# Four PSUM banks for the products of a four-layer graph network, attention weights written over the softmax tile, and three smaller edits

## The chip, the core and the metric

The kernel runs on one core of a Trainium2 chip. Five engines with queues of their own work side by side: TensorE (PE) multiplies into PSUM, VectorE (DVE) and ScalarE (ACT) read PSUM and work on SBUF, GpSimd (POOL) works on SBUF alone, and SyncE (SP) issues the DMA transfers. [...] Each queue is worked off in order, so an instruction that waits holds up all that stand behind it on its engine.

The metric is the device time of one execution in microseconds (us). One execution was also recorded by the hardware profiler.

## The reference

The input `x` is 128 graphs of 64 nodes with 512 features, with one 64x64 adjacency `adj` for all. Four layers follow each other; each is `x = x + f(relu(layernorm(x)))`:

```
L0: softmax(q kT / 8 + mask) v                       8 heads of 64
L1: (softmax(q kT / 8 + mask) v) Wo + bo             8 heads of 64
L2: rel = adj.T * (q kT); rel / ||rel|| over j; rel v    one head of 512
L3: o = (softmax(masked q kT / 8) v) Wp + bp;  o + layernorm(o)
```

All arithmetic is float32. Nearly all of it is in the projections of 512x512 weights.

## The kernel before

**Tiles.** The 8192 rows are worked in 16 tiles of 512 rows per layer, 64 tiles in all; `n` counts them through the four layers. Between layers the rows go through DRAM.

**Projections (`projection`, lines 526 to 565).** A 512x512x512 projection is seven products of half size (a Strassen scheme) where the plain way has eight. The sums of weight blocks are made once per weight (`load_w`, `sums_w`, lines 343 to 363), those of the activation, `S` and `SO`, once per tile (`sums_x`, line 497, mostly on POOL). One product is four matmuls, 128x128 by 128x256. A float32 matmul is two passes and so two rows in the trace: a product is eight rows. The seven products stand in the order 1, 6, 5, 2, 7, 3, 4 and use four PSUM tiles ("homes"): products 1 and 2 the first, 6 and 7 the second, 5 and 3 the third, 4 the fourth. Products 2, 7 and 3 add onto what is in their home, after the first of the pair has been read once. The readers are ACT copies (`s1`, `z5`, `Y11`) and DVE additions (`u2`, `u3`, `Y12`, `Y21`); POOL makes `Y22` from SBUF.

**PSUM (lines 287 to 289).** [...] The homes turn through a ring of three tiles of a bank, `ps_mm` (names `mm` in the profile). Scores and attention products have two tiles of two banks (`so`). One bank, `ps_t` (`t`), is for the warm-up, the matrix folding and layer 2's `relate`. A ring (`Ring`, line 196) hands out its tiles in turn, and a user waits until the readers of the former user of that tile are done.

**Attention (`attend`, `finish0`, `finish13`).** Two score tiles `s` per `n` go through mask and maximum (DVE), subtraction (POOL), exponential (ACT), sum (DVE) and scaling (POOL). They are then transposed by `turn` (line 447): DVE splits the float32 values into two 16-bit planes, `zp`; a transposing DMA writes `hp`; ACT puts the planes together, here into `aT`. The normalised input takes the same way into `hT`. `zp` is a ring of four tiles, `hp` of three, `s` and `aT` of two each, and `z` (used in `fold` and in `tail3`, the layer norm of layer 3's output) of two.

**Start.** 22 transposes of the identity (`WARM`, line 302) run on PE while the first rows load. The first tile (`n == 0`, lines 478 to 487) is transposed on PE, in four groups of four, one for each 128 rows.

**Folding (`fold`, lines 404 to 426).** From n = 3 on the matrices of layer 2 are folded (`Wq.T Wk` and the transposed `Wv`) in pieces between the other work; the raw weights come in three loads of 1 MB.

**End.** The last tile's output projection is done as plain matmuls, four tiles of 128 rows (lines 1060 to 1080), each followed by its layer norm and store.

**What sets the order.** The code doesn't issue instructions. `Plan` (line 56) records steps with their reads, writes and an estimated duration (line 225); generators such as `attend` are advanced one step per product by a clock of ticks (`spawn`, `tick`, `run`, lines 936 to 953). `Plan.order` (line 131) then plays the steps through: when an engine is free it takes, of the steps that are ready, the one recorded first, with those that read an `mm` tile counted as 60 steps earlier (`RUSH`). The result is the fixed order of each engine's queue. All instructions are issued in line 193, so the profile names that line for all of them, and groups are told apart by their tiles.

Of the kernel before, what the change touches and what calls it, by code (L numbers as in the profile page):

```python
# [18 lines left out]
P = 128  # L19
# [240 lines left out]
def gnn_stack_kernel(  # L260
# [17 lines left out]
    def pool(name, bufs, **kw):  # L278
        return Ring(ctx.enter_context(tc.tile_pool(name=name, bufs=1, **kw)), bufs)
# [4 lines left out]
    rows = pool("rows", 3)  # L284
    sm = pool("sm", 4)
    dram = ctx.enter_context(tc.tile_pool(name="dram", bufs=1, space=bass.MemoryType.DRAM))
    ps_mm = pool("ps_mm", 3, space=bass.MemoryType.PSUM)
    ps_so = pool("ps_so", 2, space=bass.MemoryType.PSUM)
    ps_t = pool("ps_t", 1, space=bass.MemoryType.PSUM)


    ident = const.tile([P, P], F32, tag="ident", name="ident")
# [4 lines left out]
    gps.memset(mhalf, -0.5)  # L297


    pw = ps_t.tile([P, KC, P], F32, tag="t", name="pw")  # L300
    for i in range(WARM):
        pe.transpose(pw[:, i % KC, :], ident, ident)

# [39 lines left out]
    def load_w(name, src):  # L343

        w = wp.tile([P, 7, 2, H2], F32, tag="w", name=name)
        b12 = p2.tile([P, 2, H2], F32, tag="b12", name=f"b12_{name}")

        def part(i, j):
            return src[i * H2 : (i + 1) * H2, j * H2 : (j + 1) * H2].rearrange("(c p) f -> p c f", p=P)

        dma(w[:, W11], part(0, 0))
        dma(w[:, W21], part(1, 0))
        dma(b12, part(0, 1))
        dma(w[:, W22], part(1, 1))
        return w, b12

    def sums_w(w, b12, eng):
        tt = eng.tensor_tensor
        tt(w[:, WT1], b12, w[:, W11], ALU.subtract)
        tt(w[:, WT2], w[:, W22], w[:, WT1], ALU.subtract)  # L360
        yield 1
        tt(w[:, WT4], w[:, W21], w[:, WT2], ALU.subtract)
        tt(w[:, WT3], w[:, W22], b12, ALU.subtract)

    W = {}

    def weight(name, src, eng=gps):
        got = load_w(name, src)
        W[name] = got[0]
        yield 4  # L370
        yield from sums_w(*got, eng)

    def now(gen):
        for _ in gen:
# [23 lines left out]

    def raw(tag, src, nm):
        t = p1.tile([P, KC, D], F32, tag=tag, name=nm)  # L400
        dma(t, src.rearrange("(c p) f -> p c f", p=P))
        return t

    def fold():

        rq, rk = raw("oT", wq2, "rq"), raw("SO", wk2, "rk")
        yield 8
        for dc in range(KC):
            pa = ps_t.tile([P, D], F32, tag="t", name=f"pfa_{dc}")
            plan.begin()  # L410
            for ec in range(KC):
                pe.matmul(pa, rq[:, ec, ts(dc, P)], rk[:, ec, :], start=(ec == 0), stop=(ec == KC - 1))
            plan.end()
            f = p2.tile([P, D], F32, tag="z", name=f"fa_{dc}")
            act.copy(f, pa)
            yield 1
            dma(a2d[dc * P : (dc + 1) * P, :], f)
            yield 1
        rv = raw("oT", wv2, "rv")
        yield 8  # L420
        for ec in range(KC):
            f = p2.tile([P, KC, P], F32, tag="z", name=f"ft_{ec}")
# [24 lines left out]
    def turn(dst, src, nm):  # L447


        zp = p4.tile([P, 2, D], U16, tag="zp", name=f"zp_{nm}")  # L450
        dve.tensor_copy(zp, src.bitcast(U16).rearrange("p (f w) -> p w f", w=2))
        hp = p3.tile([P, 2, KC, P], U16, tag="hp", name=f"hp_{nm}")
        plan.sync.dma_start(
            hp.rearrange("p w c t -> p (w c) t"), zp.rearrange("p w f -> p (w f)"), transpose=True
        )
        act.copy(dst.bitcast(U16).rearrange("p c (t w) -> p w c t", w=2), hp)

    def layer_norm(n):
        mv = sm.tile([P, NT, 2], F32, tag="mv", name=f"mv_{n}")
        rs = sm.tile([P, NT], F32, tag="rs", name=f"rs_{n}")  # L460
        nb = sm.tile([P, NT], F32, tag="nb", name=f"nb_{n}")

        def scales(at):
            pow_mhalf(rs[:, at], mv[:, at, 1], LN_EPS, f"{n}")
            dve.scalar_tensor_tensor(nb[:, at], mv[:, at, 0], -1.0, rs[:, at], ALU.mult, ALU.mult)

        for t in range(NT):
            stats(mv, t, xins[n][t], f"{n}")
            if n == 0:
                scales(slice(t, t + 1))  # L470
            if t % 2:
                yield 1
        if n:
            scales(slice(0, NT))
        yield 2
        hT = p2.tile([P, KC, T], F32, tag="hT", name=f"hT_{n}")
        hTs[n] = hT
        if n == 0:
            for t in range(NT):
                z = xins[n][t]  # L480
                act.activation(z, z, AF.Relu, bias=nb[:, t : t + 1], scale=rs[:, t : t + 1])
                pt = ps_mm.tile([P, KC, P], F32, tag="mm", name=f"pz_{n}_{t}")
                plan.begin()
                for c in range(KC):
                    pe.transpose(pt[:, c, :], z[:, ts(c, P)], ident)
                plan.end()
                (dve.tensor_copy if t else act.copy)(hT[:, :, ts(t, P)], pt)
        for t in range(NT) if n else ():
            z = xins[n][t]
            act.activation(z, z, AF.Relu, bias=nb[:, t : t + 1], scale=rs[:, t : t + 1])  # L490
            turn(hT[:, :, ts(t, P)], z, f"{n}_{t}")
            yield 1
        del xins[n]
        ready.add(("h", n))
        sums_of(n)
# [146 lines left out]
    def attend(n, qT, kT, v, done):  # L642
# [2 lines left out]
        plan.begin()  # L645
        psss = [scores(qT, kT, g, f"{n}_{g}") for g in range(2)]
        plan.end(300)
        ss = [p2.tile([P, 2 * KC, 2, G], F32, tag="s", name=f"s_{n}_{g}") for g in range(2)]
        yield 1
        for s, pss in zip(ss, psss):  # L650
            for b in range(2):
# [195 lines left out]
    def tail3(n, o):  # L847
# [111 lines left out]
    N = 4 * NB  # L959
    now(layer_norm(0))  # L960
    for name, got in zip(("q0", "k0"), first):
        W[name] = got[0]
        now(sums_w(*got, gps if name == "q0" else dve))
    now(weight("v0", wv0))
    make_masks()
    NAMES = {0: "qkv", 1: "qkv", 2: "av", 3: "qkv"}
# [6 lines left out]

    def want(name):
        spawn(weight(name, SRC[name]))

    pending = []

    def project(n):
# [5 lines left out]
        if m // NB == 1:  # L985
            run(projection(prod_N, W["o1"], sop, f"o_{m}", emit_out1(m)))
            spawn(tail1(m))
            if m == 2 * NB - 1:
                want("k3")
        else:  # L990
            ring, tag = (p1, "kT") if m < N - 2 else (wp, "w")
            o = ring.tile([P, NT, D], F32, tag=tag, name=f"o_{m}")
            run(projection(prod_N, W["o3"], sop, f"o_{m}", emit_out3(m, o)))
            spawn(tail3(m, o))

    for n in range(N):
# [50 lines left out]
        if l in (1, 3):  # L1047
            pending.append(n)
            spawn(load_xo(n), 4)
        if n == N - 4:  # L1050
            w12 = p2.tile([P, 2, H2], F32, tag="b12", name="w12")
            dma(w12, wp3[0:H2, H2:].rearrange("(c p) f -> p c f", p=P))

    while queue:
        tick()
    m = N - 1
    o3 = wp.tile([P, NT, D], F32, tag="w", name="o_last")
    mv = sm.tile([P, NT, 2], F32, tag="mv", name="mv_last")
    rs = sm.tile([P, NT], F32, tag="rs", name="rs_last")
    for t in range(NT):  # L1060
# [16 lines left out]
        a = p2.tile([P, D], F32, tag="z", name=f"a_last_{t}")  # L1077
# [38 lines left out]
```

## Time and profile before

| | |
|---|---|
| time, median of 3 runs | 2850.17 us (2849.34 to 2850.48) |
| the profiled execution's own time | 2849.34 us |
| its span, first to last instruction | 2847.6 us |
| busy: PE, DVE, POOL, ACT | 2829.3, 2039.3, 1847.4, 1246.9 us |
| one 128x256 pass on PE (group mean, with its pipeline) | 380 ns |
| DVE `zp<-s` / `zp<-xin` copy | 1488 / 979 ns, 188 and 252 of them |
| DVE `u<-mm,s` addition out of PSUM | 689 ns, 414 of them |
| transposing DMA `hp<-zp` | 444 issues, 3.1 us from issue to landing |

Passes on PE overlap, so the mean duration of one is longer than the time from one to the next. 168 passes that follow each other without a break take 36.53 us in the chain of waits: 0.217 us each. A product, eight passes, is thus 1.73 us. A wait is read as "who <- whom: total, times, longest". Windows of the span are given in us from its start.

### The profile page before, as it was taken

The page shows a single profiled execution, that of the slowest core. Times are in us where ns is not written, and L with a number is a line of the kernel's source. Part 1 is how long each engine was busy: PE and PEld are TensorE (multiplying, and loading weights), DVE is VectorE, ACT ScalarE, POOL GpSimd, SP SyncE. Part 2 cuts the span into 40 slices and gives each one's busy share as a digit, 9 for nine tenths or more (in the row PEclk, how much of TensorE's full clock was granted, in tenths as well). Part 3 has the DMA queues.
Part 4 walks back from the last instruction along what each step waited for, and adds up shares of the span by engine and source line. Part 5 has one row for each costly group of instructions (what it writes and reads, how often), then busy time and mean ns, then how long its engine had stood idle before and what let it go on. Part 6 is the DMA issues. An engine that isn't in the chain of part 4 may idle for free.

```text
span 2847.6 us, 61907 instructions
## 1 busy us (share of the span) xinstructions
PE 2829.3 (99%) x25822; PEld 2469.7 (87%) x25822; DVE 2039.3 (72%) x3104; ACT 1246.9 (44%) x1589; POOL 1847.4 (65%) x1349
## 2 busy tenths in 40 slices
PE   9999999999999999999999999999999999999998
PEld 8888888888888888888888888888888888888887
DVE  7677778877767667667666555555688788788787
ACT  4545555554443533534534443343444444444342
POOL 6456666656766667667677434344678688687786
PEclk9999999999999999999999999999999999999999
DMA  6666656556443433533546565656433433533531
GB/s 150 162 156 147 140 143 136 123 136 159 108 116 79 122 98 82 130 86 86 139 114 152 138 160 145 163 131 153 118 87 96 115 83 90 127 86 87 115 86 64
DMA packets 634746, 342.28 MB, mean 120 GB/s; under 512 B 485089, under 2 KB 566241, under 8 KB 634465
## 3 DMA queue, kind: packets, MB, share of 16 engines
q1 hardware_dynamic: 634464, 338.32, 49.1%
q8 instruction: 202, 3.31, 0.5%
q14 instruction: 80, 0.65, 0.1%
HBM read 152.61 MB, written 69.21 MB: 78 GB/s over the span
## 4 chain that ended last, share of the span: by engine, by line
PE 96%; DVE 2%; POOL 1%; issue 1%; DMA 0%; ACT 0%; POOLq 0%; DVEq 0%
PE mm L193 86%; PE so L193 8%; PE t L193 2%; DVE z L193 1%; DVE zp L193 0%; DVE st L193 0%; DVE xo L193 0%; POOL s L193 0%; DVE kT L193 0%; DMA hp<-zp 0%; DVE u L193 0%; POOL S L193 0%; DVE sr L193 0%; DMA xin<-in_x_dram 0%; DVE w L193 0%
## 5 line engine op out<-in xcount | busy, mean ns | idle before, releaser
L193 PE MATMUL mm<-S,w 128*128 128x256 f32 x3584 | 817.3, 380 | 3.7 <-DVE kT L193 1.3
L193 PEld LDWEIGHTS mm<-S,w 128*128 128x128 f32 x3584 | 678.2, 190 | 98.7 <-issue 2.6
L193 PE MATMUL mm<-hT,w 128*128 128x256 f32 x2688 | 631.8, 380 | 1.2 <-ACT xin L193 0.8
L193 DVE TENSOR_TENSOR u<-mm,s 128x512 f32<-128x512 f32 x414 | 285.2, 689 | 459.3 <-PE mm L193 303.8
L193 PEld LDWEIGHTS mm<-hT,w 128*128 128x128 f32 x2688 | 510.3, 190 | 72.1 <-ACT xin L193 1.0
L193 PE MATMUL mm<-w,S 128*128 128x256 f32 x2048 | 472.8, 381 | 1.9 <-DVE kT L193 1.4
L193 PEld LDWEIGHTS mm<-w,S 128*128 128x128 f32 x2048 | 385.2, 190 | 56.5 <-DVE kT L193 2.2
L193 ACT COPY hT<-hp 128x1024 uint16<-128x1024 uint16 x252 | 333.6, 1348 | 77.7 <-DMA hp<-zp 77.5
L193 PE MATMUL mm<-w,hT 128*128 128x256 f32 x1536 | 366.0, 381 | 0.0
L193 ACT COPY s<-mm 128x512 f32<-128x512 f32 x207 | 120.6, 583 | 523.8 <-PE mm L193 444.4
L193 POOL TENSOR_TENSOR s<-s,mx 128x1024 f32<-128x1024 f32 x96 | 184.4, 1922 | 239.6 <-DVE mx L193 239.5
L193 PEld LDWEIGHTS mm<-w,hT 128*128 128x128 f32 x1536 | 289.3, 190 | 41.2 <-ACT v L193 0.8
L193 ACT COPY aT<-hp 128x1024 uint16<-128x1024 uint16 x188 | 253.1, 1352 | 158.9 <-DMA hp<-zp 158.6
L193 POOL TENSOR_TENSOR xo<-xo,row 128x512 f32<-128x512 f32 x192 | 286.8, 1512 | 4.3 <-DMA xo<-x 4.3
L193 DVE COPY zp<-s 128x1024 uint16<-128x1024 uint16 x188 | 275.5, 1488 | 4.0 <-POOL s L193 3.8
L193 DVE COPY zp<-xin 128x1024 uint16<-128x1024 uint16 x252 | 242.7, 979 | 40.0 <-ACT xin L193 34.5
L193 ACT ACTIVATE xin<-xin,nb,rs 128x512 f32<-128x512 f32 x256 | 196.0, 808 | 97.5 <-DVE nb L193 93.6
L193 PE MATMUL mm<-w,SO 128*128 128x256 f32 x992 | 224.5, 379 | 0.0
L193 POOL TENSOR_TENSOR qT<-u,z 128x512 f32<-128x512 f32 x64 | 89.7, 1402 | 190.4 <-DVE u L193 172.7
L193 PEld LDWEIGHTS mm<-w,SO 128*128 128x128 f32 x992 | 188.4, 190 | 25.6
L193 POOL TENSOR_TENSOR s<-s,sr 128x1024 f32<-128x1024 f32 x96 | 187.5, 1965 | 24.3 <-DVE sr L193 23.3
L193 POOL TENSOR_TENSOR S<-hT 128x512 f32<-128x512 f32 x126 | 162.1, 1286 | 42.2 <-ACT hT L193 42.1
(109 smaller groups left out, 3623.6 us busy)
## 6 DMA issues: line engine op xcount, KB each, us to landing
xin<-x SPq DMA_DIRECT2D x192, 256.0 KB, 3.9
xo<-x SPq DMA_DIRECT2D x64, 512.0 KB, 5.2
xin<-in_x_dram SPq DMA_DIRECT2D x64, 256.0 KB, 3.1
x<-xo SPq DMA_DIRECT2D x64, 256.0 KB, 2.5
x<-xo SPq DMA_DIRECT2D x128, 128.0 KB, 2.5
x<-xo SPq DMA_DIRECT2D x32, 512.0 KB, 3.0
out_dram<-xo SPq DMA_DIRECT2D x30, 512.0 KB, 3.0
xo<-in_x_dram SPq DMA_DIRECT2D x32, 256.0 KB, 3.3
```

What stands on the lines that cost most here:

```text
L193: getattr(getattr(self.nc, eng), op)(*a, **k)
```

## The change

1. `ps_t` is gone and `ps_mm` has four tiles. The warm-up, `fold` and `relate` take theirs from this ring too.
2. `aT` is gone: the transposed weights are written over the softmax tile `s` they came from; `s` has four tiles. `relate`'s two tiles are the halves of one `s` tile.
3. `zp` is gone: `turn` takes its 16-bit planes from the ring `z`, which has four tiles and also serves `fold`, `tail3` and the end.
4. `b12` is gone: the upper right quarter of a weight is loaded where the block `WT3` will stand, and that block is computed in place. At the end, where that quarter is needed once more, it is loaded into a fifth part of the weight tile that takes tile N-2's output (`spare`).
5. `fold` loads each raw matrix in four quarters, three ticks apart.
6. After the second group of the first tile's transposes, 11 more transposes of `xin` are recorded, with a result that nobody reads. In the order that comes out, ten of them stand between the first and the second group and one between the second and the third; the third group now precedes the first product.

```
-    ps_mm = pool("ps_mm", 3, space=bass.MemoryType.PSUM)
+    ps_mm = pool("ps_mm", 4, space=bass.MemoryType.PSUM)
     ps_so = pool("ps_so", 2, space=bass.MemoryType.PSUM)
-    ps_t = pool("ps_t", 1, space=bass.MemoryType.PSUM)
...
-    pw = ps_t.tile([P, KC, P], F32, tag="t", name="pw")
+    pw = ps_mm.tile([P, KC, P], F32, tag="mm", name="pw")
...
-        dma(b12, part(0, 1))
+        dma(w[:, WT3], part(0, 1))
...
-        tt(w[:, WT1], b12, w[:, W11], ALU.subtract)
+        tt(w[:, WT1], w[:, WT3], w[:, W11], ALU.subtract)
...
-        tt(w[:, WT3], w[:, W22], b12, ALU.subtract)
+        tt(w[:, WT3], w[:, W22], w[:, WT3], ALU.subtract)
...
-        dma(t, src.rearrange("(c p) f -> p c f", p=P))
+        for c in range(KC):
+            dma(t[:, c, :], src[c * P : (c + 1) * P, :])
+            yield 3
...
-            pa = ps_t.tile([P, D], F32, tag="t", name=f"pfa_{dc}")
+            pa = ps_mm.tile([P, D], F32, tag="mm", name=f"pfa_{dc}")
...
-            f = p2.tile([P, D], F32, tag="z", name=f"fa_{dc}")
+            f = p4.tile([P, D], F32, tag="z", name=f"fa_{dc}")
...
-        zp = p4.tile([P, 2, D], U16, tag="zp", name=f"zp_{nm}")
+        zp = p4.tile([P, D], F32, tag="z", name=f"zp_{nm}").bitcast(U16).rearrange("p (w f) -> p w f", w=2)
...
                 plan.end()
+                if t == 1:
+                    for i in range(WARM // 2):
+                        pe.transpose(pw[:, i % KC, :], xins[n][0][:, ts(i % KC, P)], ident)
...
-        ss = [p2.tile([P, 2 * KC, 2, G], F32, tag="s", name=f"s_{n}_{g}") for g in range(2)]
+        ss = [p4.tile([P, 2 * KC, 2, G], F32, tag="s", name=f"s_{n}_{g}") for g in range(2)]
...
-            aT = p2.tile([P, 2, KC, P], F32, tag="aT", name=f"aT_{n}")
+            aT = s.rearrange("p (q c) b j -> p q c (b j)", q=2)
...
-            a = p2.tile([P, D], F32, tag="z", name=f"a_{n}_{t}")
+            a = p4.tile([P, D], F32, tag="z", name=f"a_{n}_{t}")
...
-        prt = ps_t.tile([P, D], F32, tag="t", name=f"pr_{n}")
+        prt = ps_mm.tile([P, D], F32, tag="mm", name=f"pr_{n}")
...
-            rel = p2.tile([P, NT, G], F32, tag="s", name=f"rel_{n}")
-            sq = p2.tile([P, NT, G], F32, tag="aT", name=f"sq_{n}")
+            both = p4.tile([P, 2, NT, G], F32, tag="s", name=f"rel_{n}")
+            rel, sq = both[:, 0], both[:, 1]
...
+    def spare(m):
+
+        t = wp.tile([P, 5, D], F32, tag="w", name=f"o_{m}")
+        return t[:, :NT, :], t[:, NT, :].rearrange("p (c f) -> p c f", c=2)
...
+                o, W["o3_12"] = spare(m)
+                dma(W["o3_12"], wp3[0:H2, H2:].rearrange("(c p) f -> p c f", p=P))
...
-    o3 = wp.tile([P, NT, D], F32, tag="w", name="o_last")
+    o3, w12 = spare(m)[0], W["o3_12"]
```

More of the change, by code (lines that the diff above doesn't have):

```diff
@@ L345, in load_w @@
         w = wp.tile([P, 7, 2, H2], F32, tag="w", name=name)
-        b12 = p2.tile([P, 2, H2], F32, tag="b12", name=f"b12_{name}")
         def part(i, j):
@@ L352, in load_w, with sums_w @@
         dma(w[:, W21], part(1, 0))
-        dma(b12, part(0, 1))
+        dma(w[:, WT3], part(0, 1))
         dma(w[:, W22], part(1, 1))
-        return w, b12
-    def sums_w(w, b12, eng):
+        return w
+    def sums_w(w, eng):
         tt = eng.tensor_tensor
-        tt(w[:, WT1], b12, w[:, W11], ALU.subtract)
+        tt(w[:, WT1], w[:, WT3], w[:, W11], ALU.subtract)
         tt(w[:, WT2], w[:, W22], w[:, WT1], ALU.subtract)
@@ L362, in sums_w @@
         tt(w[:, WT4], w[:, W21], w[:, WT2], ALU.subtract)
-        tt(w[:, WT3], w[:, W22], b12, ALU.subtract)
+        tt(w[:, WT3], w[:, W22], w[:, WT3], ALU.subtract)
     W = {}
     def weight(name, src, eng=gps):
-        got = load_w(name, src)
-        W[name] = got[0]
+        W[name] = load_w(name, src)
         yield 4
-        yield from sums_w(*got, eng)
+        yield from sums_w(W[name], eng)
     def now(gen):
@@ L400, in raw @@
         t = p1.tile([P, KC, D], F32, tag=tag, name=nm)
-        dma(t, src.rearrange("(c p) f -> p c f", p=P))
+        for c in range(KC):
+            dma(t[:, c, :], src[c * P : (c + 1) * P, :])
+            yield 3
         return t
     def fold():
-        rq, rk = raw("oT", wq2, "rq"), raw("SO", wk2, "rk")
-        yield 8
+        rq = yield from raw("oT", wq2, "rq")
+        rk = yield from raw("SO", wk2, "rk")
+        yield 4
         for dc in range(KC):
-            pa = ps_t.tile([P, D], F32, tag="t", name=f"pfa_{dc}")
+            pa = ps_mm.tile([P, D], F32, tag="mm", name=f"pfa_{dc}")
             plan.begin()
@@ L418, in fold @@
             yield 1
-        rv = raw("oT", wv2, "rv")
-        yield 8
+        rv = yield from raw("oT", wv2, "rv")
+        yield 4
         for ec in range(KC):
-            f = p2.tile([P, KC, P], F32, tag="z", name=f"ft_{ec}")
+            f = p4.tile([P, KC, P], F32, tag="z", name=f"ft_{ec}")
             turn(f, rv[:, ec, :], f"v2_{ec}")
@@ L961, in gnn_stack_kernel @@
     for name, got in zip(("q0", "k0"), first):
-        W[name] = got[0]
-        now(sums_w(*got, gps if name == "q0" else dve))
+        W[name] = got
+        now(sums_w(got, gps if name == "q0" else dve))
     now(weight("v0", wv0))
@@ L990, in project @@
         else:
-            ring, tag = (p1, "kT") if m < N - 2 else (wp, "w")
-            o = ring.tile([P, NT, D], F32, tag=tag, name=f"o_{m}")
+            if m < N - 2:
+                o = p1.tile([P, NT, D], F32, tag="kT", name=f"o_{m}")
+            else:
+                o, W["o3_12"] = spare(m)
+                dma(W["o3_12"], wp3[0:H2, H2:].rearrange("(c p) f -> p c f", p=P))
             run(projection(prod_N, W["o3"], sop, f"o_{m}", emit_out3(m, o)))
@@ L1049, in gnn_stack_kernel @@
             spawn(load_xo(n), 4)
-        if n == N - 4:
-            w12 = p2.tile([P, 2, H2], F32, tag="b12", name="w12")
-            dma(w12, wp3[0:H2, H2:].rearrange("(c p) f -> p c f", p=P))
     while queue:
@@ L1076, in gnn_stack_kernel @@
         dve.tensor_tensor(xo, xo, o, ALU.add)
-        a = p2.tile([P, D], F32, tag="z", name=f"a_last_{t}")
+        a = p4.tile([P, D], F32, tag="z", name=f"a_last_{t}")
         dve.scalar_tensor_tensor(a, o, mv[:, t, 0:1], R["gam"], ALU.subtract, ALU.mult)
```

## The prediction, made before the changed kernel ran

> **What bounds the kernel now.** I read the page's first part, its chain by engine, then PE's waits, then windows by stage.
>
> ```profile
> PE 2829.3 (99%) x25822; PEld 2469.7 (87%) x25822; DVE 2039.3 (72%) x3104; ACT 1246.9 (44%) x1589; POOL 1847.4 (65%) x1349
> ...
> PE 96%; DVE 2%; POOL 1%; issue 1%; DMA 0%; ACT 0%; POOLq 0%; DVEq 0%
> ```
>
> PE is the bound; no other engine is over 72%. The change takes no product away, so all that it can win is time in which PE stands still or runs slowly. PE is idle 2847.6 − 2829.3 = 18.3 us. Where, the windows tell (columns: window and its length, then busy us of PE, PEld, DVE, ACT, POOL, then clock and DMA):
>
> ```profile
> 0.00:60.00 60.00, 56.76 (x377) 49.02 (x378) 41.80 (x76) 23.52 (x34) 37.75 (x41) 0.97 0.69 163
> 60.00:750.00 690.00, 689.57 (x7046) 597.36 (x7045) 524.95 (x786) 358.33 (x458) 422.39 (x294) 1.00 0.62 142
> 750.00:1520.00 770.00, 770.00 (x7100) 675.40 (x7099) 527.65 (x760) 328.31 (x423) 533.04 (x385) 1.00 0.43 106
> ...
> 2250.00:2800.00 550.00, 544.89 (x5108) 476.23 (x5108) 448.82 (x619) 232.63 (x287) 429.88 (x306) 1.00 0.40 99
> 2800.00:2848.00 48.00, 38.12 (x302) 33.24 (x301) 38.66 (x57) 8.16 (x13) 30.29 (x25) 0.94 0.12 45
> ```
>
> From 60 to 2250 us PE loses 0.4 us. There is something to win in three places only: the start (and there also a clock below 1.00), layer 3 from 2250 us, and the last 48 us. What PE waits for outside the start:
>
> ```profile
> PEld mm L193 <- DVE kT L193: 3.9, 3, 1.7
> PEld mm L193 <- POOL kT L193: 1.6, 1, 1.6
> PEld mm L193 <- ACT z L193: 0.8, 1, 0.8
> PEld mm L193 <- DVE u L193: 0.8, 1, 0.8
> ```
>
> Every one ends when a reader of a PSUM home is done, so these are waits for a home to come free, not for data. Measured as the time between two starts of a pass on PE beyond 0.216 us, the stalls between 40 and 2700 us are 0.59 (at 44.8), 0.17 (265.7), 0.57 (443.1), 0.17 (714.4), and in layer 3 0.79 (2260.7), 1.47 (2291.4), 1.07 (2398.6), 0.50 (2505.2), 1.51 (2611.3), 0.97 (2690.3): 7.8 us. The 1.47 in rows:
>
> ```profile
> 2287.35 3.42 DVE L193 COPY zp<-s 128x1024 uint16<-128x1024 uint16 x2
> ...
> 2290.70 1.75 DVE L193 SCALAR_TENSOR_TENSOR z<-kT,mv,row 128x512 f32<-128x512 f32 x1
> ...
> 2292.37 0.68 DVE L193 TENSOR_TENSOR kT<-mm,kT 128x512 f32<-128x512 f32 x1
> ...
> 2293.10 3.07 PE L193 MATMUL mm<-S,w 128*128 128x256 f32 x13 [1.30 <-DVE kT L193]
> ```
>
> The reader `kT<-mm,kT` (`Y21`) stood in DVE's queue behind two copies and a slow norm instruction; PE's next product had to wait for its bank.
>
> **1, four homes: −7.8 us.** With a ring of three a home takes the tile that the home three hand-outs earlier had, so one or two products lie between the last write of the old home and the first write of the new. With four, each of a projection's homes follows its own predecessor, and at least one product more lies between: 8 × 0.216 = 1.73 us. The longest stall is 1.51 us, below 1.73, so each of the ten fits into the added slack. One thing more: in layer 3's q projections the planner of before placed product 5 behind 2 and 7, since its home wasn't free, which left one product between 6 and 7; the stalls at 2398.6, 2505.2 and 2611.3 are product 7 waiting for `u2` in its own home. In the new order 5 and 2 stand between them again, +1.73 us, above 1.07, 0.50 and 1.51. Ends: −7.8, and 0 if the readers come later by as much. I take the full −7.8: sizes and places are both in rows. Late next is the reader itself: one over 1.7 us later than today shows again. `relate` and `fold` now take tiles of the same ring, one more hand-out; `relate` sits in 1520 to 2250 us, where no PE wait is seen and DVE (54%, then 76% busy) and ACT (40%, 42%) have room. Cost 0; without that cover, one product's wait for a reader, 1.5 us as above, for some tile.
>
> **6, the fill: −1.0 us.** The first tile's rows (columns: start, duration):
>
> ```profile
> 6.43 0.66 PE L193 MATMUL mm<-ident,xin 128*128 128x128 f32 x4 [0.39 <-ACT xin L193]
> ...
> 7.30 0.66 PE L193 MATMUL mm<-ident,xin 128*128 128x128 f32 x4 [0.21 <-ACT xin L193]
> ...
> 8.78 3.51 PE L193 MATMUL mm<-hT,w 128*128 128x256 f32 x8 [0.83 <-ACT xin L193]
> ```
>
> The clock records show 1.0 from 5.62 to 9.03, 0.5 from 9.03 to 12.45, then 1.0. So the first product's eight passes take 3.31 us (8.78 to 12.09, 0.41 each) where 1.73 would do: 1.6 us lost after a stretch in which PE stood 0.39 + 0.21 + 0.83 us and was busy (5.4 to 8.8) 1.97 of 3.4 us. Each transpose takes 0.109 us, eleven 1.2 us, about the 1.43 that PE stands. In the new order: group 0 at 6.43, ten fills, group 1 at 7.95 (0.65 later), one fill, group 2 when its rows are normalised (8.42), the DVE copy of group 1 (0.69 after the group's start, 0.69 long) done at 9.33, product 1 at 9.43, warm, to 11.16, group 3, product 2 at 11.6 where it was at 13.14. Product 5 needs `S`, two DVE additions of 0.69 behind the hT copies: 13.35 instead of 15.07. That is −1.7; if the clock halves all the same, the later start costs +0.6. Against the whole −1.7 speaks the next tile: its `S` additions on POOL were just in time (last one at 51.6, its product at 52.6), so part is eaten by waiting for POOL. Between −1.7 and what 1.0 us of slack leaves I take −1.0.
>
> [...] 22 identity transposes alone (1.34 to 6.0) preceded the granted 1.0, so in this trace transposes count as work. [...]
>
> **End: −1.0 us.** After PE's last pass (2838.38) the span runs 9.2 us on DVE:
>
> ```profile
> 2838.78 0.68 DVE L193 TENSOR_TENSOR w<-mm,row 128x512 f32<-128x512 f32 x1
> ...
> 2840.23 0.75 DVE L193 SCALAR_TENSOR_TENSOR xo<-z,rs,xo 128x512 f32<-128x512 f32 x1
> 2840.90 0.69 DVE L193 BATCH_NORM_STATS2 st<-w 128x6 f32<-128x512 f32 x1
> ...
> 2843.50 0.75 DVE L193 SCALAR_TENSOR_TENSOR xo<-z,rs,xo 128x512 f32<-128x512 f32 x1 [0.46 <-POOL rs L193]
> ```
>
> Between the last `w` and its statistics stand `z` and `xo` of the tile before (2839.39 to 2840.98). With four `z` tiles the order puts that `z` ahead of the last `w` and the statistics right behind it: one 0.74 and its gap of 0.1 less in the chain, and `w`, which started 0.4 after PE's last pass, up to 0.2 sooner: −1.0 (0 if the moved `z` holds up `w` by as much; −1.3 if the gap before the last row goes too).
>
> **2, 3, 5, the shared `z` and `s` tiles: +1.5 us.** `zp` had four tiles for itself; now `a` of `tail3`, `fold` and the splits turn through four. In layer 3 the first `a` of a tile takes what the first split of `s` filled: between them DVE does by its rows `u` 0.69, `kT` 0.69, a split 1.49, three statistics 0.67, two 0.18: 5.2 us, and the transposing DMA lands 3.1 us after issue; no wait. In layer 0, while `fold` holds two of the tiles, the same tile is rewritten after 4.1 and once after 1.7 us against 3.1: DVE waits some 0.7 and 1.4 us, and behind it in the queue stands `u3`, the reader that a product waits for; PE's cover there is three products, 5.2 us. Before, DVE already waited 3.5 us for these DMAs (longest 1.3) without PE feeling it. Ends: 0, and in layer 3, where DVE is at 82%, far more (rival D). I take one stall of the longest kind seen, 1.5. Softmax's `s` as the target: `s` is read by the split before the ACT copy writes it, and four tiles stand for two and two; 0. Quarters: 12 loads of 256 KB for 3 of 1 MB, nine more issues of about 0.5 us on SP's queue, by three ticks apart; 256 KB loads land in 2.7 to 5.1 us by the page's DMA part, the 1 MB one in 9.0, and fold's products are no one's input before layer 2 (1520 us). They are queued on SP among row loads and stores, whose consumers are a whole tile away; 0, else one row load late by 0.5.
>
> **4, `b12`: 0.** Four loads as before, one POOL or DVE operation in place. `v0`'s load no longer waits for `q0`'s sums to free `b12`; its sums on POOL come earlier. Weights come a layer ahead; without that cover, one POOL operation, 1.3 us. The last quarter's load is issued at the output of N−2 instead of N−4's step, a tile (40 us) before its use; landing as above.
>
> **Sum.** −7.8 − 1.0 − 1.0 + 1.5 = −8.3 against the profiled run: 2849.34 − 8.3 = 2841.0. The median stands 0.83 above that run: **2841.9 us**. A measurement of this kernel can tell about 0.2% (5.7 us) from no change.
>
> **Rivals.**
> B, the clock halves anyway: the fill ends before 8.4 us, and the wait for the copy before product 1 remains. +0.6 for −1.0: −6.7, 2843.5.
> C, the change doesn't do what it says: the stalls come back as late readers or as waits for `S` on POOL (78% busy in layer 3) because a PE that is ahead meets the same DVE. For it: DVE is 82% and the longest stall sits behind long copies. Against it: PE as a whole is the bound, and a stall that is cured doesn't make DVE's work more. Bank term 0: −0.5, 2849.7.
> D, slower: DVE tied to the transposing DMAs in layer 3 through the shared ring. It begins when a DMA lands later than DVE's 5.2 us of work plus the 5.2 us of slack of three products, some 10 us after the split. For it: three such DMAs in a row took 9.37 us of SP's queue at 2607.35; against it the median 3.1. From about 1.0 us in each of the 16 tiles (15.5 us) it decides; at 1.5 us, +24 less what A wins, 2849.34 + 24 − 9.8 + 0.8 = 2864.
>
> **How the numbers follow.** A 0.58, B 0.08, C 0.20, D 0.14. A's own range is 2838.2 to 2844.5: down, −7.8 − 1.7 − 1.3 = −10.8, and the 1.2 us of PE's waits for ACT copies of `v` and `oT`; up, a third of the bank term (2.6) not won. The range given leaves out D alone: 2838.2 to 2852.3, the upper end being C with a halved clock and no gain at the end (0 + 0.6 + 0 + 1.5). Faster by 0.2% is below 2844.5: A and B, 0.66. Within: C, 0.20. Slower: D, 0.14.
>
> **What would show it.** Banks: no PE wait on `kT`, `u` or `z` of over 0.3 us between 2250 and 2800 us, and PE busy over 549 of the 550 us. Fill: clock 1.0 at 9 us and the first product in 1.73 us. End: under 8.5 us from PE's last pass to the span's end. Shared ring: DVE's waits for `hp<-zp`, 3.5 us before, under 8. I am wrong if these grow to tens, or if PE waits for `S` or `hT` in layer 3.

## The result, and the profile after

| | before | changed |
|---|---|---|
| median of 17 runs each | 2849.55 us (2848.17 to 2851.90) | 2844.49 us (2843.95 to 2845.48) |
| the profiled execution's own time | 2849.34 us | 2844.57 us |
| its span | 2847.6 us | 2842.8 us |
| last pass on PE to the end of the span | 9.2 us | 7.8 us |

The ratio is 0.9982, with a 95% interval of 0.9974 to 0.9989: faster by 5.1 us, 0.18%, where −8.3 us had been forecast. It lies inside the range given and inside the likeliest case's own range, at its upper end, just short of the 0.2% mark.

The changed kernel's page, busy times and chain by engine:

```profile
PE 2828.4 (99%) x25833; PEld 2471.6 (87%) x25833; DVE 2037.6 (72%) x3104; ACT 1248.0 (44%) x1589; POOL 1840.5 (65%) x1349
...
PE 96%; DVE 3%; issue 0%; POOL 0%; DMA 0%; ACT 0%; POOLq 0%; SPq 0%; DVEq 0%
```

PE is still the bound and does the same work, but for the eleven transposes. Its windows (window and length, busy us of PE, PEld, DVE, ACT, POOL, then clock, DMA share, GB/s):

```profile
0.00:60.00 60.00, 58.09 (x396) 50.96 (x397) 44.36 (x77) 24.20 (x35) 38.12 (x41) 1.00 0.65 154
60.00:750.00 690.00, 690.00 (x7052) 598.96 (x7051) 524.43 (x784) 360.89 (x460) 419.22 (x293) 1.00 0.64 144
750.00:1520.00 770.00, 769.39 (x7096) 675.06 (x7095) 530.30 (x762) 325.50 (x421) 536.02 (x386) 1.00 0.44 105
...
2250.00:2795.00 545.00, 541.29 (x4983) 473.68 (x4975) 438.58 (x616) 231.15 (x285) 425.49 (x305) 1.00 0.41 100
2795.00:2843.00 48.00, 39.61 (x307) 34.10 (x305) 40.67 (x58) 8.17 (x13) 33.16 (x26) 0.96 0.12 45
```

The first 60 us have their clock at 1.00 and 1.3 us more PE work in them, and 60 to 750 us have no gap left. (The clock column counts from the first clock record on, here 6.58 us, and shows 1.00 ahead of it. In both kernels the transposes start 0.213 us apart before the first record and 0.109 after it, so they come at about half the rate until then.) But layer 3 still loses 3.7 us of 545, and 750 to 1520 us, which lost nothing before, loses 0.6. PE's waits (what waits, for whom: total, times, longest):

```profile
PE mm L193 <- DVE kT L193: 3.7, 4, 0.9
...
PE so L193 <- issue: 0.6, 1, 0.6
```

Both traces hold the same 11656 projection passes, so the k-th of one can be set against the k-th of the other and the difference of their starts followed. Where score groups are placed earlier or later the difference jumps by about 2 us and back, by more while the matrices are folded; what is left, in us:

| where | moved by |
|---|---|
| first tile | −1.2 |
| old waits for homes gone at 44.8, 265.7, 443.1, 714.4 | −0.6, −0.3, −0.7, −0.3 |
| a gap in the middle of a score group at 752 us | +0.9 |
| six old waits in layer 3 gone | −6.6 |
| four new waits in layer 3, at 2398, 2505, 2612, 2719 | +4.8 |
| another order in the last tile | +0.6 |
| after the last pass | −1.4 |
| sum (measured by the spans: −4.8) | −4.8 |

The gap at 752 us is 0.61 us long and stands inside a run of 128 score matmuls; the waits answer shows it as `issue`, that is with no releaser. So the old waits are gone as forecast, and more than half of that gain is lost to four new ones. One of them, in rows of the changed kernel's timeline (start, duration, engine, operation; in brackets the idle time before and its releaser):

```profile
2606.50 1.72 POOL L193 TENSOR_TENSOR kT<-u,row 128x512 f32<-128x512 f32 x1
...
2608.36 1.64 DVE L193 SCALAR_TENSOR_TENSOR z<-kT,mv,row 128x512 f32<-128x512 f32 x1
...
2609.92 1.75 DVE L193 COPY z<-s 128x1024 uint16<-128x1024 uint16 x1
...
2611.60 0.68 DVE L193 TENSOR_TENSOR kT<-mm,kT 128x512 f32<-128x512 f32 x1
...
2612.33 1.99 PE L193 MATMUL mm<-hT,w 128*128 128x256 f32 x8 [0.93 <-DVE kT L193]
```

`kT<-mm,kT` is `Y21` of an output projection (`emit_out3`). Its input from POOL, `kT<-u,row`, is there at 2608.22, but in DVE's queue the layer norm's `a` (`z<-kT`) and a split of `s` stand ahead of it, so it starts 3.4 us later. PE waits because the planner put product 4 of the next q projection ahead of product 3 in this tile, and product 4 takes the home that `Y21` still has to read. Each of the four costs 1.09 us beyond the usual 0.216 from pass to pass, and the pass behind it comes another 0.10 late: 1.2 us in all.

### The profile page after: what moved, and what is told of

Its sections match the earlier page's. It is cut to its first block, busy times and chain, and to the rows that moved or that the text cites. A ratio compares the mean times of both kernels' runs of the same rounds, so it can differ in the third digit from the quotient of the medians.

```text
span 2842.8 us, 62036 instructions
## 1 busy us (share of the span) xinstructions
PE 2828.4 (99%) x25833; PEld 2471.6 (87%) x25833; DVE 2037.6 (72%) x3104; ACT 1248.0 (44%) x1589; POOL 1840.5 (65%) x1349
## 3 DMA queue, kind: packets, MB, share of 16 engines
q8 instruction: 202, 3.31, 0.5%
## 4 chain that ended last, share of the span: by engine, by line
PE 96%; DVE 3%; issue 0%; POOL 0%; DMA 0%; ACT 0%; POOLq 0%; SPq 0%; DVEq 0%
PE mm L193 88%; PE so L193 8%; DVE z L193 1%; DVE st L193 0%; POOL s L193 0%; DVE u L193 0%; DVE sr L193 0%; DVE kT L193 0%; DMA xin<-in_x_dram 0%; DVE mv L193 0%; DVE w L193 0%; DVE xo L193 0%; ACT xin L193 0%; ACT oT L193 0%; POOLq L1120 0%
## 5 line engine op out<-in xcount | busy, mean ns | idle before, releaser
L193 ACT COPY s<-hp 128x1024 uint16<-128x1024 uint16 x188 | 252.3, 1352 | 204.3 <-DMA hp<-z 197.1
L193 DVE COPY z<-s 128x1024 uint16<-128x1024 uint16 x188 | 278.2, 1501 | 6.7 <-POOL s L193 6.6
L193 DVE COPY z<-xin 128x1024 uint16<-128x1024 uint16 x252 | 245.3, 988 | 37.6 <-ACT xin L193 34.0
L193 ACT ACTIVATE s<-s 128x1024 f32<-128x1024 f32 (+1 forms) x112 | 108.1, 966 | 200.3 <-POOL s L193 144.3
```

Source lines behind the costliest of these rows:

```text
L193: getattr(getattr(self.nc, eng), op)(*a, **k)
```

## The experiments

Times are medians; each ratio is taken against the kernel before on the same chip (2849.65, 2849.38 and 2848.74 us on the three chips used). In each table row and text below, "waits in layer 3" is the time between starts of two 128x256 passes beyond 0.216 us, summed over those above 0.3 us between 2250 and 2750 us.

| kernel | us | waits in layer 3 | after the last pass |
|---|---|---|---|
| before | 2849.55 | 6.1 (6 places) | 9.2 |
| changed | 2844.49 | 4.4 (4) | 7.8 |
| banks_only | 2846.24 | 0 | 10.1 |
| three_banks | 2854.84 | 11.3 (10) | 7.8 |
| own_a | 2841.88 | 0 | 9.8 |
| own_zp | 2841.95 | 0 | 9.8 |
| third_first | 2840.18 | 0 | 7.8 |
| no_fill | 2846.47 | 4.4 (4) | 7.8 |
| fill_5 | 2845.53 | 4.4 (4) | 7.7 |
| with_b12 | 2845.17 | 4.4 (4) | 7.8 |
| before_fill | 2849.11 | 6.1 (6) | 9.2 |

**The fourth home alone (banks_only).** On the kernel before; the tiles `pw`, `pa` and `prt` come from `ps_mm`.

```
-    ps_mm = pool("ps_mm", 3, space=bass.MemoryType.PSUM)
+    ps_mm = pool("ps_mm", 4, space=bass.MemoryType.PSUM)
-    ps_t = pool("ps_t", 1, space=bass.MemoryType.PSUM)
...
```

> The kernel before with part 1 of the change alone (ring of four homes, warm-up, folding and relate in it). Theory: the fourth home takes away the ten old waits (7.8 us), but in layer 3 the planner now places product 4 ahead of product 3 in six q projections, and each of these waits about 1.1 us for Y21 of the output projection, whose home it takes (the change as a whole has four such places at 1.09). So 2849.5 - 7.8 + 6.6 = about 2848.3, with a first product at half clock and 9.2 us after the last pass as before. Rival: the new waits come from the shared z and s tiles, not from the order; then they are absent here and the time is 2849.5 - 7.8 = 2841.7.

Measured: 2846.24 us (2844.61 to 2847.99), ratio 0.9988 (0.9978 to 0.9997). Between the two expectations, but the trace decides: layer 3 has no wait for a home at all. From the waits of PE in this kernel:

```profile
PE mm L193 <- ACT v L193: 1.7, 1, 1.7
...
PE mm L193 <- DVE S L193: 1.0, 1, 1.0
PE so L193 <- POOL v L193: 0.8, 1, 0.8
```

My theory that product 4 ahead of product 3 makes the wait falls: the planner's order has it in six tiles here, and none waits. The rival holds for layer 3: the new waits come with the other parts. That the kernel doesn't reach the rival's 2841.7 lies elsewhere: 1.0 us for `S` at 14 us, 0.5 at 41, 1.7 for a copy of `v` at 131 while the matrices are folded (and 0.5 at 133), and 10.1 us after the last pass.

**The other parts without the fourth home (three_banks).** On the changed kernel; `pw`, `pa` and `prt` come from `ps_t`.

```
-    ps_mm = pool("ps_mm", 4, space=bass.MemoryType.PSUM)
+    ps_mm = pool("ps_mm", 3, space=bass.MemoryType.PSUM)
+    ps_t = pool("ps_t", 1, space=bass.MemoryType.PSUM)
...
```

> The changed kernel with part 1 undone (three homes, a bank of its own for warm-up, folding and relate). Theory: the start (-1.3) and the end (-1.4) stay, the waits for homes of the kernel before come back in number and kind (DVE kT and u, 6 to 8 us between 40 and 2700 us, against 4.4 in the changed kernel): 2847 to 2848.5. Rival: the parts 2 to 5 are what moved the waits and the banks are worth nothing: 2844.5.

Measured: 2854.84 us (2854.13 to 2855.73), ratio 1.0019 (1.0009 to 1.0028): slower than the kernel before, and worse than either side had said. PE's waits in it:

```profile
PE mm L193 <- DVE kT L193: 9.7, 10, 1.3
PE mm L193 <- DVE u L193: 1.7, 2, 1.3
```

The waits don't merely come back, they nearly double. Together with the kernel before, the fourth home alone and the changed kernel this makes a square of the waits in layer 3: three homes 6.1 with the old rings and 11.3 with the new, four homes 0 and 4.4. The fourth home is worth 6 to 7 us there, and the other parts cost 4 to 5 us there, with either number of homes. Outside layer 3 this kernel has four more waits of over 0.5 us, 3.6 us in all, which the changed kernel doesn't have.

**Which of the other parts: a ring of its own for `a` (own_a).** On the changed kernel, in `tail3`:

```
-            a = p4.tile([P, D], F32, tag="z", name=f"a_{n}_{t}")
+            a = p2.tile([P, D], F32, tag="a", name=f"a_{n}_{t}")
```

> The changed kernel with one ring more: the tile a of layer 3's layer norm comes from a ring of two of its own, as before the change, and all else of z stays shared. The order that comes out has Y21 of the output projection one place behind its input in DVE's queue, where the changed kernel has it behind a and a split in every second tile (3.4 us late). Theory (four z tiles let a become ready earlier and slip ahead of Y21): the four waits of 1.09 us vanish although the planner still puts product 4 ahead of 3, 2844.5 - 4.4 = 2840.1. Rival (product 4 ahead of 3 makes the wait, whatever DVE does): six such places now, 2844.5 + 2 = 2846.7.

Measured: 2841.88 us (2841.39 to 2842.47), ratio 0.9974 (0.9964 to 0.9984). The four waits are gone. The same tile as above, in this kernel's timeline:

```profile
2603.88 1.72 POOL L193 TENSOR_TENSOR kT<-u,row 128x512 f32<-128x512 f32 x1
...
2606.07 0.68 DVE L193 TENSOR_TENSOR kT<-mm,kT 128x512 f32<-128x512 f32 x1
...
2607.09 1.89 PE L193 MATMUL mm<-S,w 128*128 128x256 f32 x8
...
2608.81 1.89 PE L193 MATMUL mm<-hT,w 128*128 128x256 f32 x8
```

`Y21` follows its input by 0.47 us, and the product that stands ahead of product 3 starts 1.72 us after the one before it, without a wait. That `a` shares the ring of the splits is thus the cause: in the changed kernel two steps `a` (2605.65 and 2608.36) stand ahead of `Y21`, here one (2601.07) does and the next comes behind it. In the tile with the wait at 2398 us DVE works in the same order and at the same times within 0.03 us in both kernels from 2383 to 2391 us; there they part (rows of DVE, three of the changed kernel and then two of this one):

```profile
2391.51 0.66 DVE L193 BATCH_NORM_STATS2 st<-xin 128x6 f32<-128x512 f32 x1
2392.09 1.43 DVE L193 SCALAR_TENSOR_TENSOR z<-kT,mv,row 128x512 f32<-128x512 f32 x1
...
2394.79 1.65 DVE L193 SCALAR_TENSOR_TENSOR z<-kT,mv,row 128x512 f32<-128x512 f32 x1
```

```profile
2391.49 2.01 DVE L193 SCALAR_TENSOR_TENSOR a<-kT,mv,row 128x512 f32<-128x512 f32 x1
...
2395.64 0.77 DVE L193 COPY z<-s 128x1024 uint16<-128x1024 uint16 x1
```

Why, the planner's own times tell; played through, its code gives DVE's order of either trace, instruction for instruction. In the changed kernel the first `a` of this tile takes the `z` that the first split filled. The planner estimates that the DMA which reads it lands at 2376.47 us of its own time, 0.98 us after this `a` could start otherwise (2375.49). So a statistics step of the next input goes first, and DVE comes free at 2379.34 where it is 2379.93 with a ring for `a`. The third split is ready at 2379.89: in the changed kernel DVE doesn't wait for it and takes the second `a`, and the split and `Y21` move back. The second `a` isn't ready sooner in the shared ring, it is ready later (2378.39 for 2376.20). With a ring of its own it comes behind the splits all the same, since they were recorded earlier. On the chip the DMA isn't late: ACT reads `hp` from 2390.25 on, ahead of the first `a` at 2392.09. The other three tiles with a wait go alike. In the planner's times a ring of four for `a` alone, or one of six for all users of `z`, also leaves only one `a` ahead of `Y21`. So what counts is that `a` and the splits share four tiles, and not that the ring of `a` grew; no run has such a ring.

The time is 1.8 us above the 2840.1 expected, because the order at the end changed too: the last layer norms stand one behind the other on DVE again, and 9.8 us follow the last pass where the changed kernel has 7.8. PE's last pass is 4.5 us earlier, as expected.

**Part 3 undone altogether (own_zp).** On the changed kernel; `fold`, `a` and the end take their `z` from `p2`.

```
-        zp = p4.tile([P, D], F32, tag="z", name=f"zp_{nm}").bitcast(U16).rearrange("p (w f) -> p w f", w=2)
+        zp = p4.tile([P, D], F32, tag="zp", name=f"zp_{nm}").bitcast(U16).rearrange("p (w f) -> p w f", w=2)
...
-            a = p4.tile([P, D], F32, tag="z", name=f"a_{n}_{t}")
+            a = p2.tile([P, D], F32, tag="z", name=f"a_{n}_{t}")
```

> The changed kernel with part 3 undone: a ring of four for the splits, a ring of two for fold, a and the end. Theory: layer 3 as in the kernel with a ring of its own for a (no waits, -4.4), and the end's order as before the change (+1.4 after the last pass): 2841.5. Rival: the end's gain isn't from the z ring but from the load of the last quarter: then 2840.1.

Measured: 2841.95 us (2841.14 to 2842.21), ratio 0.9973 (0.9963 to 0.9984): 2841.5 was expected. No waits in layer 3, and 9.8 us after the last pass. So the end's gain of the change is owed to the shared ring, but not to the end's own tile alone, which own_a leaves shared.

**Product 4 kept behind product 3 (third_first).** On the changed kernel, in `projection`; `Q3` holds the names of layer 3's q projections.

```
             plan.end()
+            if nm in Q3 and i == 3:
+                third = len(plan.steps) - 1
+            elif nm in Q3 and i == 4:
+                plan.steps[-1][2].add(third)
```

> The changed kernel with one order more: in the q projections of layer 3 product 4 may not be placed ahead of product 3. In four of these projections the planner then puts k's product 1, then q's 3, then q's 4. Theory (the place in the order makes the four waits of 1.09 us): they vanish, 2844.5 - 4.4 = 2840.1. Rival (the reader Y21 is late whatever stands there): the next product that needs a late reader waits instead, here k's product 1 for the copy Y11 or q's 4 again, and the time stays within 1 us of 2844.5.

Measured: 2840.18 us (2839.67 to 2840.36), ratio 0.9966 (0.9953 to 0.9979): the expected 2840.1, and the fastest of all, 9.5 us below the kernel before. Here `Y21` is as late as in the changed kernel, but no product waits at its home yet (rows of this kernel's timeline):

```profile
2393.32 1.72 POOL L193 TENSOR_TENSOR kT<-u,row 128x512 f32<-128x512 f32 x1
...
2396.33 1.89 PE L193 MATMUL mm<-S,w 128*128 128x256 f32 x8
2396.74 1.76 DVE L193 COPY z<-s 128x1024 uint16<-128x1024 uint16 x1
2398.05 1.89 PE L193 MATMUL mm<-hT,w 128*128 128x256 f32 x8
2398.42 0.68 DVE L193 TENSOR_TENSOR kT<-mm,kT 128x512 f32<-128x512 f32 x1
```

PE starts the product at 2398.05 (now k's product 1) while `Y21` begins at 2398.42. Both are needed for the wait: a late `Y21`, and a product on its home early. Taking either away removes it.

**Without the fill (no_fill).** On the changed kernel:

```
-                if t == 1:
-                    for i in range(WARM // 2):
-                        pe.transpose(pw[:, i % KC, :], xins[n][0][:, ts(i % KC, P)], ident)
```

> The changed kernel without the eleven fill transposes. Theory: the clock halves again at 9 us, the first product takes 3.3 us, and the time is 2844.5 + 1.3 = 2845.8, everything after 60 us shifted alike. Rival: the fill only takes the place of idle time and the next tiles' wait for their S ends where it did: 2844.5, the difference gone by 60 us.

Measured: 2846.47 us (2844.83 to 2847.62), ratio 0.9987 (0.9978 to 0.9997), 2.0 us above the changed kernel and with a spread of 2.8 us for 1.5. In its profiled execution the clock is at half not for 3.4 us, as in the kernel before, but for 6.8 us, from 8.36 to 15.18. Its windows answer:

```profile
7.00:9.00 2.00, 0.88 (x4) 0.54 (x4) 1.16 (x5) 1.75 (x3) 1.57 (x4) 0.84 1.10 312
9.00:11.00 2.00, 1.17 (x4) 0.96 (x4) 1.59 (x2) 0.54 (x2) 1.52 (x2) 0.50 0.95 234
11.00:13.00 2.00, 2.00 (x6) 1.56 (x5) 0.00 (x0) 0.53 (x1) 1.92 (x2) 0.50 0.90 264
13.00:15.00 2.00, 2.00 (x10) 1.80 (x9) 0.47 (x1) 0.59 (x1) 1.59 (x2) 0.50 1.08 116
```

The second to last column is the DMA share, the one before it the clock. Everything behind is shifted by about 3 us in this execution, with the same four waits. In the changed kernel the same windows read:

```profile
7.00:9.00 2.00, 1.79 (x18) 1.55 (x15) 1.14 (x4) 1.92 (x3) 1.53 (x5) 1.00 1.06 269
9.00:11.00 2.00, 2.00 (x11) 1.80 (x12) 1.85 (x3) 0.71 (x1) 1.92 (x2) 1.00 1.04 307
```

**Five transposes for eleven (fill_5).** On the changed kernel:

```
-                    for i in range(WARM // 2):
+                    for i in range(5):
```

> The changed kernel with five fill transposes for eleven. Theory (the clock is granted by how busy PE is in the stretch before; a run without fill shows it at half from 8.7 to 15 us in one execution and not at all in others): the first product is at half clock in part of the executions, the times spread over some 2 us, median 2844.5 to 2846. Rival (any fill is enough, or the order of the groups does it): 2844.5 with the spread of the changed kernel, 1.5 us.

Measured: 2845.53 us (2844.37 to 2847.02), ratio 0.9987 (0.9978 to 0.9996): a spread of 2.7 us. Median and spread lie between the changed kernel and the one without fill, but the theory's reason, that the clock goes by how busy PE was in the stretch before, isn't shown. The profiled execution (2845.38 us) has the clock at 1.00 from 4.10 us on and still loses 1.7 us on the changed kernel's by 52 us: 0.5 at product 5, where PE waits 0.9 for `S`, and 1.2 where PE waits for `hT`. It gets 0.9 back, since the gap at 752 us is absent. All ten executions have a mean granted clock of 0.999 or 1.000, where seven of the ten without fill have 0.998.

**The fill alone (before_fill).** On the kernel before, the tile `pw` being that of `ps_t`:

```
+                if t == 1:
+                    for i in range(WARM // 2):
+                        pe.transpose(pw[:, i % KC, :], xins[n][0][:, ts(i % KC, P)], ident)
```

> The kernel before with the eleven fill transposes of part 6 alone. Theory (the fill keeps the clock at full speed in every execution, where without it the clock halves for a window or two in some): the times lose their upper part, the median falls by 1.3 to 2 us from 2849.4 to about 2847.8, and the spread from 4 to about 1.5 us; the waits of layer 3 stay as in the kernel before, 6.3 us. Rival (the fill helps only together with the fourth home, since the warm-up's tile, the four groups and the first product need five tiles): 2849.4 with the spread as before.

Measured: 2849.11 us (2848.68 to 2849.72) against 2848.74 (2847.80 to 2852.16) of the kernel before on that chip, ratio 0.9998 (0.9989 to 1.0008). The spread falls from 4.4 to 1.0 us as expected; the median does not fall. The clock is 1.00 from its first record at 4.15 us on, the first product takes its 1.73 us, and product 5 starts 0.9 us earlier than in the profiled execution of before, whose clock was at 0.50 from 9.03 to 12.45 us. Of this 0.15 goes at 44 us (the wait for `z` there grows from 0.59 to 0.74) and 0.64 at 181 us, again in the middle of a score group and without a releaser (timeline of this kernel):

```profile
178.66 2.07 PE L193 MATMUL so<-kT,qT 64*64 64x64 f32 x122
...
181.05 0.34 PE L193 MATMUL so<-kT,qT 64*64 64x64 f32 x6 [0.32 <-issue]
```

The lower runs of before (2847.8 to 2848.7) are faster than the median with the fill. An estimate from the trace says why: had the clock not halved in the profiled execution of before, where the first product's passes took 3.31 us for 1.73, it would have been 1.6 us shorter, 2847.7. The fill puts the second group of transposes 0.65 us later, so by this estimate it costs time where the clock would have stayed up, and saves some where it would have halved.

**The weight quarter in a tile of its own again (with_b12).** On the changed kernel, in `load_w` and `sums_w`; the end's load stays as changed.

```
+        b12 = p2.tile([P, 2, H2], F32, tag="b12", name=f"b12_{name}")
...
-        dma(w[:, WT3], part(0, 1))
+        dma(b12, part(0, 1))
...
-        tt(w[:, WT1], w[:, WT3], w[:, W11], ALU.subtract)
+        tt(w[:, WT1], b12, w[:, W11], ALU.subtract)
...
-        tt(w[:, WT3], w[:, W22], w[:, WT3], ALU.subtract)
+        tt(w[:, WT3], w[:, W22], b12, ALU.subtract)
```

> The changed kernel with the weight quarter loaded into b12 again (a ring of two, as before), the end left as changed. Theory (I had costed the missing b12 at nothing, and the kernel with four banks alone loses 2 to 3 us between 13 and 45 us waiting for the sums of v0's weight): v0's quarter waits for q0's sums, its sums come late and PE waits for them near 40 us: 2845.5 to 2847. Rival (b12 is as good as nothing): 2844.5.

Measured: 2845.17 us (2844.28 to 2845.29), ratio 0.9984 (0.9974 to 0.9993); PE's last pass is 0.2 us later than in the changed kernel's trace, and PE doesn't wait for a weight near 40 us. That is 0.7 us by the medians and 0.2 by the traces (0.7 there too but for the gap at 752 us, which is 0.5 us smaller in this one); my theory, at least 1 us, falls. What delays the first tiles and the folding in the kernel with the fourth home alone is thus not settled; parts 3, 5 and 6 are left for it.

## Why the prediction was right or wrong

**Four homes, −7.8: right.** All ten waits named are gone, −8.4 by the traces (−1.8 and −6.6; the forecast left out the 0.1 us by which the pass behind a wait is late), and the four-home kernels with the old ring for `a` have none in layer 3. The reason given, one product more of slack, held, and "late next is the reader itself: one over 1.7 us later than today shows again" is what came: `Y21` 3.4 us behind its input. I wrote that sentence and put no price on it. So the sign named for the banks did not come: PE waited four times for `kT` in layer 3, 0.9 us each, and was busy for 541.3 of 545 us.

**The fill, −1.0: right for the pair of traces, wrong as a fixed worth.** The first tile won 1.2 us (product 1 at 9.47 where 9.43 was forecast, at full clock; product 5 at 13.9 to 14.0 where 13.35 was, since product 2 had to wait for the copy `s1` and a DVE copy). Taken out of the changed kernel it costs 2.0 us, put into the kernel before it gives nothing in the median. The step that failed is the 1.6 us "lost" to the half clock in the kernel before, taken as a property of the program. It is one of the single execution, and the first thing that the fill takes away is the spread.

Transposes alone went with the full clock in two more traces, as they did in that of the kernel before. The changed kernel fills the stretch from 6.58 to 9.47 us with transposes alone, PE busy for 2.68 us of 2.89, and its clock stays at 1.00; without the fill it fell to 0.50 at 9.03 us in the profiled execution of the kernel before and at 8.36 us in that of no_fill, and stayed at 1.00 in that of banks_only. With the fill alone (before_fill) the first record of the full clock, at 4.15 us, comes after 13 transposes and nothing else. From PE's first pass until the clock fell the longest gap was 1.2 us in no_fill and 0.83 us in the kernel before.

**The end, −1.0: right,** −1.4, with the order that was named (timeline of the changed kernel):

```profile
2835.06 0.69 DVE L193 TENSOR_TENSOR w<-mm,row 128x512 f32<-128x512 f32 x1
2835.78 0.69 DVE L193 BATCH_NORM_STATS2 st<-w 128x6 f32<-128x512 f32 x1
2836.39 0.73 DVE L193 SCALAR_TENSOR_TENSOR xo<-z,rs,xo 128x512 f32<-128x512 f32 x1
...
2838.91 0.75 DVE L193 SCALAR_TENSOR_TENSOR xo<-z,rs,xo 128x512 f32<-128x512 f32 x1 [0.46 <-POOL rs L193]
```

The statistics follow the last `w` at once; `xo` of the tile before comes after them.

**The shared rings, +1.5: the term that was mis-sized.** New waits and orders measured +6.3 in all: 4.8 in layer 3, which own_a puts down to the shared ring, and 0.9 at 752 us and 0.6 in the last tile, which no run puts down to it. The step that was wrong is "no wait" for the first `a` in layer 3, behind the DMA of the first split. On the chip it is right: DVE's whole wait for those DMAs is smaller than before, 3.1 for 3.5 us, as the changed kernel's waits show:

```profile
DVE z L193 <- DMA hp<-z: 3.1, 2, 1.7
```

But the order is made beforehand, from the planner's estimates, and there the wait exists: 0.98 us, enough to let another step go first and then the second `a` ahead of the split and `Y21`. I had costed the shared ring by the waits that it adds on the chip, and never asked what it adds in the plan. The swap of products 3 and 4 was in the listed order of the changed kernel, and I had read only the place of product 5 in it.

**The other zeros.** `b12`: 0.2 to 0.7 us. Quarters of the folded matrices and the softmax tile as target: no wait on them is seen in the trace of the changed kernel; neither was undone by itself. For the gap at 752 us, 0.61 us of idle time and 0.9 us in all, I had no term; what speaks for its cause stands in the last section, and no run varied it.

**The rivals.** C named the mechanism (late readers, longest behind long copies) and gave it the whole bank term; it took 4.8 of 8.4. B is not in the trace of the changed kernel. D did not come: DVE's whole wait for the DMAs is 3.1 us. That C stood at 0.20 with its price all or nothing was the weak point; a middle value was the likeliest.

## What to carry to other kernels

Where a planner fixes the order, a shared ring is also an order: each wait that sharing adds in the plan can change the order, even one that the chip would never feel. For each ring that gets a new user, look in the planner's times for steps that start later than before, which step takes their place, and which reader then comes later; and read in the new order not only the step that was expected to move but every step that takes a tile whose reader is late. When the bound engine loses its time to such readers, the cheap cure is to keep the consumer of the late tile behind another that is ready: here one added dependency was worth 4.3 us, almost as much as the whole change. A change of several parts is best judged by a square of two parts at a time, since here the parts cancelled each other.

## What the runs showed of the hardware that was not expected

The half clock at the start differs from one execution to the next. The kernel before ran 67 times on the three chips of the experiments: the 23 executions with a mean granted clock of 0.998 took 2849.6 to 2852.2 us, the 44 with 0.999 took 2847.8 to 2850.5. (The mean also holds the clock of 0.50 after PE's last pass, in the kernel before from 2842.1 us to the end, so it tells the two apart only in the main.) The half clock of the start lasts 3.41 us in the trace of the kernel before, from 9.03 us, and twice that in the one without fill, from 8.36 us. In the 3.41 us ahead of it PE was busy for 1.97 us (58%) and 1.66 us (49%). The first row here is of the kernel before, from the windows answer:

```profile
5.62:9.03 3.41, 1.97 (x13) 1.29 (x12) 2.51 (x8) 3.00 (x5) 2.54 (x6) 1.00 1.09 320
9.03:12.45 3.42, 3.42 (x10) 2.60 (x10) 0.00 (x0) 0.69 (x2) 3.26 (x3) 0.50 1.10 300
```

With the fourth home alone, without fill, PE was busy for 1.96 us (57%) of the 3.41 us from 6.72 to 10.13, because the first product already fell into them, and the clock stayed at 1.00. With eleven transposes it was busy for 2.37 us (before_fill, from 4.15) to 3.20 us (the changed kernel, from 6.58) of such a stretch, and the clock was at 1.00 from there until after PE's last pass in every trace. The spreads go with it: 4.4, 2.8 and 3.4 us without fill, 0.7 to 1.6 us in the seven kernels with eleven transposes. So the clock stayed up at 57% in one trace and fell at 58% in another; what decides it these traces do not show.

The second thing are gaps inside a run of score matmuls for which the trace has no releaser. Seven traces have one such group of 128 passes, which takes 0.35 to 0.94 us longer than the usual 2.02: at 752 to 756 us in the changed kernel (0.93), third_first (0.94), own_a, with_b12, own_zp and no_fill (0.35), and at 181 us in before_fill. The order of the tiles isn't the cause, since fill_5 has the changed kernel's order there and no gap. The gaps have one thing in common: counted by their starts, PE has begun 15041 instructions ahead of the gap in six traces and 3265 in before_fill, which is 46 × 256 fewer. In no_fill, whose program is 21 instructions shorter by then, the gap stands 21 instructions later in the program and at the same count. The page has 202 packets of 16 KB on the queue `q8` (kind `instruction`) for some 51800 instructions of PE, which would be about 256 to a packet. In each of the seven a packet of `q8` began 2.25 to 2.51 us before PE went on. In the traces without a gap at that count it began 2.39 us (fill_5) to 4.2 us before. That speaks for a wait for PE's next instructions; no run varied their loading, so it is not shown.
